# A four-layer graph attention kernel: counting and ranking of neighbour lists moved between engines

## The chip, the cores and the metric

The kernel runs on one core of a Trainium2 chip. A core has five engines that run side by side, each with its own in-order queue: TensorE (PE, matrix products into PSUM), VectorE (DVE), ScalarE (ACT), GpSimd (POOL) and SyncE (SP, which here only starts transfers). The metric is the device time of one execution in microseconds (us), as the median of several runs. A lower time is better.

## The reference

Four graph attention layers run one after the other on the same node features `x` (3327 nodes, 512 features) and the same graph `adj` (a 3327x3327 integer matrix, symmetric, with ones on the diagonal and about 0.5% of ones elsewhere). Every layer is preceded by a normalisation and a residual:

```python
h = jnp.maximum(_layernorm(x, axis=-1), 0.0)
x = x + _L0_gnn_ref(h, adj, L0_gnn_W, L0_gnn_a_src, L0_gnn_a_dst)
...
# inside a layer, for each head:
h = (x @ W.T).reshape(n, Hh, d)
e = leaky_relu(e_src[:, None, :] + e_dst[None, :, :], 0.2)
e = jnp.where(mask[:, :, None], e, -jnp.inf)
alpha = softmax(e, axis=1)
out = jnp.einsum('ijh,jhd->ihd', alpha, h)
```

The layers have 8, 4, 1 and 8 heads. A softmax row thus runs over the few neighbours of a node, and a kernel may gather those instead of multiplying with the whole matrix.

## The kernel before

The nodes are padded to 3328 and cut into 26 tiles of 128. A first stage, which fills about the first tenth of the time, builds for every node a list of up to 40 neighbours, sorts the nodes by the length of their lists, and makes the feature rows of layer 0. The four layers then work in the sorted order: tile t of the sorted nodes has a fixed number of list places (`CAPS[t]`), gathers that many rows with indirect transfers issued by GpSimd, weights them on VectorE and adds them up on TensorE. Only the first stage is touched by the change.

**The loop of the first stage** (`for t in range(NT)`, from L692) runs over the 26 tiles of `adj`. For tile t:

- SyncE loads the 128x3328 integers of `adj` into `a` (L697; three buffers). GpSimd multiplies them by descending column numbers into `key` (L698; three buffers), so that the largest keys are the first neighbours.
- VectorE raises the diagonal (L702) and takes the eight largest of each of 16 segments into `cand` (L707). ScalarE sums the row of `a` to the list length `total` (L704), writing the unneeded values into `waste`.
- Between VectorE's 16 segment operations the pieces of the tile before are run, one after each: five times "eight largest of the candidates" (`top`, L662) and four times their removal (L664); then `counted`, then `sorted_in`. After the ninth segment operation `placed` of the tile before that is run.
- `counted(t)`: ScalarE makes list entries from `top` (L632 `kept`, L633 `L`); VectorE counts the filled places into `held` (L635, an operation with an accumulator, which shows as two instructions).
- `sorted_in(t)`: VectorE compares the count with the 41 possible counts and gets a one-hot row `o` (L640); TensorE multiplies it by an upper triangle of ones and adds the counts so far, which gives the number of earlier nodes with the same count, `pn` (L642, L643), and updates the counts so far, `count` (L645, L646); ScalarE copies those to `sofar` (L649). `pn` and `count` have one PSUM buffer each.
- `placed(t)`: VectorE multiplies `pn` by `o` and sums, so that `part` holds the node's place within its count (L654).
- The feature rows: ScalarE's queue loads the tile of `x` into one of five row buffers `vx` (L726). ScalarE computes mean, centred features `xn`, sum of squares and `ve` (`centred_by_scalar`, L488 to L495; `xn` has two buffers). One tile later `features` makes the row: TensorE transposes `xn` (L454), ScalarE cuts at zero (`hT`, L461), TensorE multiplies by the weights (`pv`, L472, one buffer, eight products that the profile shows as sixteen), GpSimd takes the inverse square root of `ve` (`root`, L434), ScalarE scales `pv` into `vx` (L683, L685), and SyncE stores it into the table `tabx` (L687).

**The order.** On GpSimd and VectorE the order is that of the program text (a manual schedule). On ScalarE, TensorE and SyncE a scheduler orders the instructions before the run. On every engine the queue is then fixed, so an instruction that waits holds all behind it. On GpSimd the root of tile t-1 stands behind the key product of tile t. After the second tile VectorE folds the attention vectors into the weights (`W.fold`, L408, L410).

**The end of the stage**, after the last tile: VectorE forms from `count` the first place of every count (`base`, L738), multiplies all one-hot rows by it (L739, 128x1066), sums (L741), adds `part` (L742) and so has every node's rank. From the rank it makes selection matrices, with which TensorE sorts the lists (L789); the index lists (L790, L791) release the first gather of layer 0. `check` compares lengths and diagonals, for a dense path that these inputs never take.

## Time and profile before

| What | Value |
|---|---|
| median of 3 runs | 2420.67 us (2420.39 to 2422.86) |
| the profiled execution | 2419.54 us, span of its instructions 2417.8 us |
| mean granted clock of TensorE | 0.953 of full speed |
| busy: PE / DVE / ACT / POOL | 2068.3 / 1885.1 / 936.3 / 1739.5 us |
| first key product, last key product start | 5.2 us, 233.80 us |
| last `top` of the stage ends, ranks ready | 251.49 us, 256.7 us |
| first gather of layer 0 starts | 271.24 us |
| key product of GpSimd (L698), each | 7.26 us |
| row sum of `adj` on ScalarE (L704), each | 2.97 us |

The profile shows one execution. A line such as `L698 POOL ...` names a line of the kernel, the engine and the operation, and then the tile that it writes and those that it reads. A time in square brackets is the time that the engine was idle before the instruction, with the instruction or transfer that ended the wait. The waits view adds these up: which engine waited for which, the total in us, how many times, and the longest. The view by stretches gives the busy time of each engine in a piece of the execution, TensorE's granted clock, the busy share of the transfer engines and the rate. PEld is TensorE's loading of weights.

### The profile page before, as it was taken

To read this page: it belongs to the slowest core of one execution; us is meant where nothing else is said; L and a number is where in the kernel's file an instruction comes from. 1 tells how busy PE (TensorE), PEld (TensorE's weight loads), DVE (VectorE), ACT (ScalarE), POOL (GpSimd) and SP (SyncE) were. 2 spreads that over 40 slices of the span, in tenths; PEclk is the share of its full clock that TensorE was granted. 3 is DMA by queue.
4 is the path that set the end of the run, shared out by engine and by line. 5 is a ranking of instruction groups with operands and counts; after the bars stand their busy time and mean duration, and the time that the engine had idled before them with its cause. 6 is when DMAs were issued, how large, how long until landed. Compare 5 with 4: busy or idle time off the path is not lost.

```text
span 2417.8 us, 27489 instructions
## 1 busy us (share of the span) xinstructions
PE 2068.3 (86%) x7298; PEld 1197.0 (50%) x7298; DVE 1885.1 (78%) x4857; ACT 936.3 (39%) x2528; POOL 1739.5 (72%) x1717
## 2 busy tenths in 40 slices
PE   2778779888988885898999987899898699999997
PEld 1656334444444432454455544456565465556653
DVE  7988788877777763888888884888878578888886
ACT  5777113434331111433333332544443444344430
POOL 7899267777777776766677772778778467777775
PEclk9988899999999997999999998999999899999999
DMA  5887569999998788887888884889887578888885
GB/s 227 316 299 248 153 192 299 276 299 282 286 283 237 234 231 241 242 245 235 234 261 255 256 237 141 270 262 283 268 248 240 161 226 256 250 243 246 252 241 176
DMA packets 260732, 594.23 MB, mean 246 GB/s; under 512 B 103699, under 2 KB 121107, under 8 KB 256214
## 3 DMA queue, kind: packets, MB, share of 16 engines
q0 software_dynamic: 124368, 432.13, 59.5%
q1 hardware_dynamic: 132454, 153.45, 19.6%
q10 hardware_dynamic: 3744, 6.82, 0.8%
q8 instruction: 59, 0.97, 0.2%
q14 instruction: 107, 0.88, 0.1%
HBM read 542.60 MB, written 49.65 MB: 245 GB/s over the span
## 4 chain that ended last, share of the span: by engine, by line
DVE 31%; DMA 17%; PE 16%; issue 13%; POOL 12%; ACT 9%; DVEq 0%; SPq 0%; ACTq 0%; POOLq 0%
DVE m L931 13%; POOL g L838 8%; DMA g<-tab,idxb 6%; PE bank L936 5%; DMA g<-tabx,twiceb 4%; PE pv L472 4%; PE whole L1173 3%; POOL key L698 3%; DVE bank L924 3%; ACT r L1280 2%; DMA g<-tab,idxa 2%; DVE room L1296 2%; DVE z L902 2%; ACT pw L903 2%; DVE z L900 1%
## 5 line engine op out<-in xcount | busy, mean ns | idle before, releaser
L936 PE MATMUL bank<-m,ident 128*128 128x512 f32 x2414 | 1128.0, 613 | 144.8 <-DVE m L931 144.3
L838 POOL DMA_INDIRECT g<-tab,idxb x712 | 683.1, 959 | 236.0 <-issue 162.0
L931 DVE TENSOR_TENSOR m<-g,pw 128x512 f32<-128x512 f32 x1207 | 752.2, 682 | 100.2 <-ACT pw L903 99.6
L936 PEld LDWEIGHTS bank<-m,ident 128*128 128x128 f32 x2414 | 448.7, 194 | 689.2 <-issue 314.6
L472 PE MATMUL pv<-w,hT 128*128 128x264 f32 x1664 | 431.5, 413 | 67.8 <-ACT hT L461 44.5
L903 ACT ACTIVATE pw<-z 128x32 f32<-128x32 f32 (+4 forms) x356 | 68.2, 191 | 988.9 <-DVE z L902 988.9
L472 PEld LDWEIGHTS pv<-w,hT 128*128 128x128 f32 x1664 | 331.7, 203 | 166.8 <-ACT hT L461 50.8
L838 POOL DMA_INDIRECT g<-tab,idxa x297 | 286.3, 964 | 165.0 <-issue 110.6
L838 POOL DMA_INDIRECT g<-tabx,twiceb x342 | 324.0, 947 | 106.0 <-issue 79.5
L1173 PE MATMUL whole<-ve,em 128*128 128x512 f32 x468 | 217.8, 612 | 16.3 <-DVE em L1152 11.2
L698 POOL TENSOR_TENSOR key<-a,keys 128x3328 int32<-128x3328 int32 (+1 forms) x29 | 189.3, 6530 | 16.3 <-DVE cand L707 11.8
L924 DVE SCALAR_TENSOR_TENSOR bank<-g,L,bank 128x512 f32<-128x512 f32 x243 | 183.3, 754 | 6.8
L900 DVE TENSOR_TENSOR z<-g,pw 128x32 f32<-128x32 f32 (+4 forms) x356 | 62.6, 176 | 152.1 <-DMA g<-tabx,twiceb 64.7
L1314 PEld LDWEIGHTS whole<-L,room 128*128 128x128 f32 x1248 | 147.5, 190 | 24.9 <-issue 19.1
L838 POOL DMA_INDIRECT g<-tabx,twicea x99 | 94.9, 959 | 78.5 <-issue 38.1
L1314 PE MATMUL whole<-L,room 128*128 128x130 f32 x1248 | 147.8, 274 | 0.0
L707 DVE MAX8 cand<-key 128x8 f32<-128x208 int32 x416 | 144.0, 364 | 0.1
L1173 PEld LDWEIGHTS whole<-ve,em 128*128 128x128 f32 x468 | 88.1, 196 | 109.2 <-issue 87.2
L1280 ACT ACTIVATE r<-low,L 128x384 f32<-128x384 f32 x208 | 121.2, 583 | 5.1
L454 PE MATMUL pt<-ident,xn 128*128 128x128 f32 x416 | 65.4, 281 | 35.4 <-ACT hT L461 13.6
L454 PEld LDWEIGHTS pt<-ident,xn 128*128 128x128 f32 x416 | 52.5, 145 | 68.6 <-issue 28.3
L931 DVE TENSOR_TENSOR bank<-g,pw 128x512 f32<-128x512 f32 x74 | 51.5, 696 | 37.4 <-ACT pw L903 36.6
(180 smaller groups left out, 2192.6 us busy)
## 6 DMA issues: line engine op xcount, KB each, us to landing
a<-in_adj SPq DMA_DIRECT2D x25, 1664.0 KB
tab<-v SPq DMA_DIRECT2D x78, 264.0 KB
ve<-tab SPq DMA_DIRECT2D x78, 264.0 KB
g<-tab SPq DMA_DIRECT2D x65, 264.0 KB
tabx<-vx SPq DMA_DIRECT2D x26, 528.0 KB
g<-tab,idxb POOLq DMA_INDIRECT x712, 4.0
low<-tab SPq DMA_DIRECT2D x52, 132.0 KB
spare<-tab SPq DMA_DIRECT2D x52, 132.0 KB
```

Of the source, the lines that this page charges most:

```text
L454: nc.tensor.transpose(pt[:, k, :], xn[:, k * P:(k + 1) * P], ident)
L472: nc.tensor.matmul(pv[:, s, :HF + 8], hT[:, k, :], W.w[:, k, s, :], start=(k == 0), stop=(k == KC - 1))
L698: nc.gpsimd.tensor_tensor(key[:, c:c + quarter], a[:, c:c + quarter], keys[:, c:c + quarter], OP.mult)
L707: nc.vector.max(cand[:, g * 8:(g + 1) * 8], key[:, g * SEG:(g + 1) * SEG])
L838: nc.gpsimd.indirect_dma_start(out=out_, out_offset=None, in_=table, in_offset=bass.IndirectOffsetOnAxis(ap=which, axis=0))
L903: nc.scalar.activation(self.wt[:, k0:k0 + n, :H], z, AF.Exp)
L924: nc.vector.scalar_tensor_tensor(acc, v, w, acc, OP.mult, OP.add)
L931: nc.vector.tensor_tensor(out_.rearrange("p (s h d) -> p s h d", s=2, d=D), v.rearrange("p s (h d) -> p s h d", d=D), wt[:, k0 + q, :H].re ...
L936: nc.tensor.matmul(self.po, ident, m[:, q, :], start=False, stop=(k0 + q == K - 1), skip_group_check=True)
L1173: nc.tensor.matmul(tl.po.rearrange("p (s m) -> p s m", s=2), e[:, q * P:(q + 1) * P], v.rearrange("p (s m) -> p s m", s=2)[:, :, :F // 2], ...
L1280: nc.scalar.activation(self.r[:, h, :], self.a[:, g, :], AF.Relu, bias=-1.0, scale=self.b[:, j, g:g + 1])
L1314: nc.tensor.matmul(dst, e[:, h, q * P:(q + 1) * P], mov, start=False, stop=(j == NT - 1), skip_group_check=True)
```

## The change

ScalarE now counts the empty places instead of VectorE counting the filled ones: a second activation of `kept` with an accumulator, between `kept` and `L`. The possible counts `bins` run upwards, so that an empty count is compared with them. `sorted_in` comes two places later among VectorE's pieces. `placed` is now a copy by ScalarE of the whole `pn` into `before`, kept for all tiles, and at the end VectorE adds `base` to `before` for all tiles in one operation (128x1066), multiplies by `o` and sums. `features` of a tile runs two tiles later instead of one, for which `xn` has three buffers; the last two tiles' rows are made after the loop.

```diff
@@ centred_by_scalar
-    xn = work.tile([P, F], F32, name="xn")
+    xn = work.tile([P, F], F32, name="xn", bufs=3)
@@ tile_gat_stack
-        held = once.tile([P, NT], F32, name="held")
-        part = once.tile([P, NT], F32, name="part")
+        empty = once.tile([P, NT], F32, name="empty")
+        before = once.tile([P, NT, BINS], F32, name="before")
...
-            nc.scalar.activation(bins, counting(BINS, -1, KMAX, 0), AF.Copy)
+            nc.scalar.activation(bins, counting(BINS, 1, 0, 0), AF.Copy)
@@ counted
             nc.scalar.activation(kept, top, AF.Relu)
+            junk = small.tile([P, KMAX], F32, name="junk")
+            nc.scalar.activation(junk, kept, AF.Relu, scale=-1.0, bias=1.0, accum_out=empty[:, t:t + 1])
             nc.scalar.activation(L[:, t, :], kept, AF.Copy, scale=-1.0, bias=float(NP))
-            junk = small.tile([P, BINS], F32, name="junk")
-            nc.vector.scalar_tensor_tensor(junk[:, :KMAX], top, 0.0, one.to_broadcast([P, KMAX]), OP.is_gt,
-                                           OP.mult, accum_out=held[:, t:t + 1])
@@ sorted_in
-            nc.vector.tensor_scalar(o[:, t, :], bins, held[:, t:t + 1], None, OP.is_equal)
+            nc.vector.tensor_scalar(o[:, t, :], bins, empty[:, t:t + 1], None, OP.is_equal)
@@ placed
-            junk = small.tile([P, BINS], F32, name="junk")
-            nc.vector.scalar_tensor_tensor(junk, pn[:, :BINS], 1.0, o[:, t, :], OP.mult, OP.mult,
-                                           accum_out=part[:, t:t + 1])
+            nc.scalar.activation(before[:, t, :], pn[:, :BINS], AF.Copy)
@@ rest
             pieces.append(lambda: counted(t, top))
+            pieces += [lambda: None] * 2
             pieces.append(lambda: made.append(sorted_in(t)))
@@ check
-            nc.vector.tensor_tensor(m1, held, total, OP.not_equal)
+            nc.vector.tensor_tensor(m1, empty, total, OP.add)
+            nc.vector.tensor_scalar(m1, m1, float(KMAX), None, OP.not_equal)
@@ the loop over tiles
-        count, pieces, last, normed = None, [], None, None
+        count, pieces, last, normed = None, [], None, []
...
-                if normed is not None:
-                    features(*normed)
-                normed = (t, vx, *centred_by_scalar(nc, xt, small, work))
-            features(*normed)
+                if len(normed) == 2:
+                    features(*normed.pop(0))
+                normed.append((t, vx, *centred_by_scalar(nc, xt, small, work)))
+            for each in normed:
+                features(*each)
@@ the end
-            nc.vector.tensor_mul(o, o, base[:, :BINS].unsqueeze(1).to_broadcast([P, NT, BINS]))
+            nc.vector.tensor_tensor(before, before, base[:, :BINS].unsqueeze(1).to_broadcast([P, NT, BINS]), OP.add)
+            nc.vector.tensor_mul(o, o, before)
             rank = small.tile([P, NT], F32, name="rank", bufs=1)
             nc.vector.tensor_reduce(rank, o, AX.X, OP.add)
-            nc.vector.tensor_add(rank, rank, part)
```

## The prediction

> **What bounds the list building now.** The change touches only the first 260 us, so I left the page's totals and read that stretch: starts of the key products on GpSimd (L698), then the waits, then the timelines of ScalarE and TensorE. The page counts 26 products of about 7.26 us (the first cut in four); with the root (L434) a period of 7.73 us is the best GpSimd can do. Yet the one of tile 5 starts at 62.84 and that of tile 25 at 233.80: 8.55 us each. The waits from 60 to 245 us say why (engine line, awaited engine line: us, times, longest):
>
> ```profile
> ACT vx L683 <- PE pv L472: 15.8, 11, 5.3
> ...
> POOL key L698 <- DVE cand L707: 11.8, 1, 11.8
> ACT sofar L649 <- PE count L646: 11.6, 12, 2.3
> POOL root L434 <- ACT ve L495: 11.4, 6, 4.6
> ACT waste L488 <- DMA vx<-in_x: 10.9, 8, 2.3
> DVE junk L654 <- PE pn L643: 8.8, 7, 2.3
> ```
>
> The 11.8 is one wait at 62.8 us, for VectorE after it folded the weights; the change leaves it. What may go are 11.4 (GpSimd's in-order queue holds the next product behind a root that ScalarE feeds late) and 8.8 (VectorE held by the pick L654). I call "round t" VectorE's work between the diagonal additions (L702) of tiles t and t+1. Rounds 2 to 6 start at 55.64, 62.68, 69.71, 76.73 and 83.77, so an unheld round takes 7.03; rounds 23 and 25 start at 225.44 and 241.10.
>
> Two things in the trace decide what a new wait costs. VectorE's two counted operations are cheap in the stream:
>
> ```profile
> 61.29 0.18 DVE L635 SCALAR_TENSOR_TENSOR junk<-top,fixed 128x40 f32<-128x40 f32 x1
> 61.39 0.09 DVE L635 DVE_READ_ACCUMULATOR junk<-top,fixed 128x1 f32 x1
> 61.39 0.38 DVE L707 MAX8 cand<-key 128x8 f32<-128x208 int32 x1
> 61.68 0.24 DVE L640 TENSOR_SCALAR o<-fixed,held 128x41 f32<-128x41 f32 x1
> ```
>
> From start to start L635 delays what follows by 0.10 us, not by the 0.27 of its durations. And TensorE's clock halves when it resumes after a pause (columns: stretch, PE, PEld, DVE, ACT, POOL busy, clock, DMA share, GB/s):
>
> ```profile
> 82.11:85.53 3.42, 0.23 (x1) 0.23 (x2) 3.42 (x18) 3.42 (x7) 3.42 (x1) 1.00 0.95 395
> 85.53:88.94 3.41, 3.41 (x12) 2.77 (x11) 2.62 (x14) 2.66 (x9) 3.13 (x3) 0.50 1.06 332
> 109.42:112.83 3.41, 3.07 (x18) 2.75 (x18) 3.41 (x18) 3.41 (x6) 3.29 (x3) 1.00 0.94 386
> ```
>
> [...] the weight products (L408) on VectorE last 6.88 and 7.36 us beside a key product, and 0.70 without.
>
> **The change, part by part.** VectorE loses L635 and L654: 0.10 us each by start-to-start, so a round takes 6.83. ScalarE gains the empty count (taken as L632's 0.23 us, plus a 0.19 accumulator read) and the copy of the prefix counts (as L649, 0.20). In the stream, where starts follow at about 0.13, 0.09 and 0.11, that is 0.33 us a tile; neither form is in the trace, so at worst it is their whole 0.62, and it can't be a gain, being added work. I take 0.33. The end work gains an addition of 128x1066.
>
> The root a tile later takes GpSimd's wait for ve away. But VectorE's one-hot (o) now waits for ScalarE's count, and what stands ahead of that count decides. The scheduler's order of the changed ScalarE queue, once steady, is:
>
> ```
> sofar, before, xn, hT, squares, waste(a), kept, vx (528), empty, L, vx (16), ve, mean of x, load x
> ```
>
> TensorE's order is: one product of pv, then pn and count, seven of pv, four transposes. Thus a ring: o -> pn, count -> sofar -> before -> xn -> hT -> squares -> waste(a) -> kept -> vx -> empty -> o. Its length, start to start, from this ScalarE row and others like it:
>
> ```profile
> 94.59 0.61 ACT L488 ACTIVATE waste<-vx 128x512 f32<-128x512 f32 x1
> 95.11 0.19 ACT L488 ACTIVATION_READ_ACCUMULATOR waste<-vx 128x1 f32 x1
> ...
> 96.79 0.21 ACT L649 ACTIVATE sofar<-count 128x41 f32<-128x41 f32 x1 [1.37 <-PE count L646]
> 96.90 0.71 ACT L490 ACTIVATE xn<-vx,nm 128x512 f32<-128x512 f32 x1
> 97.51 2.97 ACT L704 ACTIVATE waste<-a 128x3328 bf16<-128x3328 int32 x1
> 100.38 0.19 ACT L704 ACTIVATION_READ_ACCUMULATOR waste<-a 128x1 f32 x1
> 100.47 0.69 ACT L683 ACTIVATE vx<-pv,root 128x528 f32<-128x528 f32 x1
> ```
>
> ScalarE: sofar 0.10, before 0.12, xn 0.61, hT 0.48, squares 0.61, waste(a) 2.96, kept 0.13, vx 0.58: 5.59. From the empty count back to sofar there are two branches. By VectorE: 0.37 to o, 0.3 to pn, about 1.0 through count: 1.7. By TensorE: pv has one buffer, so its first product waits for vx (16), which starts 0.36 after the count; 0.32 on it begins, and pn stands behind it:
>
> ```profile
> 64.74 0.71 PE L472 MATMUL pv<-w,hT 128*128 128x264 f32 x2 [0.70 <-ACT vx L685]
> 65.29 0.31 PE L642 MATMUL pn<-o,upper 128*128 128x41 f32 x2
> ```
>
> so 0.36 + 0.32 + 0.55 + 1.03 = 2.26. The longer branch gives 5.59 + 2.26 = 7.85 us a tile at full clock, already over GpSimd's 7.73. TensorE works 5.3 of it and pauses 2.5 just before pv and pn, where half clock strikes. In the kernel before, TensorE's bursts after 64 us last 5.15 warm; of nine that follow a pause over 2.2 us seven ran at half clock (6.7 to 9.3 us), and of those after 1.76 or less none as a whole. A cold burst is 1.7 longer, so its next pause is short and the clock stays up: about every second tile is cold. Then pn to count takes 1.77 instead of 1.0 (from 191.5 us), and pv's first product up to 0.5 more. Half the tiles with 0.9 more: 0.45. Ring: 8.3. (No cold tile: 7.85; all cold: 8.75.) The mean of x sits in a 1 us hole of the ring, so a load of x of up to 8.8 us is hidden; landings here take 2.5 to 8.6.
>
> First rounds. In round 1 the count stands behind waste(a) and xn, and VectorE reaches the folding about 0.9 late; [...]: nothing [...]. In round 2 the count stands behind vx of tile 1, which waits for pv until 63.70:
>
> ```profile
> 63.70 0.70 ACT L683 ACTIVATE vx<-pv,root 128x528 f32<-128x528 f32 x1 [5.28 <-PE pv L472]
> ```
>
> o can start at 63.70 + 0.6 + 0.37 = 64.7; unheld it would at 62.15. Round 3 starts at 65.2, +2.5. Round 3 is not held: 72.0, +2.3. In round 4 the count stands behind waste(a), which waits for xn of tile 5; its load is issued at about 69, not at 66.3, and I take 5 us: x at 74, count at 80.4, round 5 at 81.2, +4.5. Round 5 is held 0.9: round 6 at 89.0, **+5.2**. (A load of 3 us: +3.5; cold TensorE: +6.5.) While VectorE is late GpSimd waits for its key buffers (three), as at 62.84: no reserve catches this.
>
> Then 17 rounds on the ring, 17 x 8.3 = 141.1, against 225.44 - 83.77 = 141.7: **-0.6**. Rounds 23 and 24 have no waste(a) left: 2 x 6.83 against 15.66: **-2.0**.
>
> The end. The last count goes by ScalarE: the last top is done at 251.49, o follows at 251.77; now 0.04 + 0.27 + 0.33 + 0.04 = 0.68 instead of 0.28: +0.4. The 1066-wide addition costs what L739 does, 1.27, with its gap 1.30; L654 and the addition of ranks go, 0.23 and 0.22 from start to start; round 25 saves 0.2: +0.65. Together **+1.05**. One more small operation of the check fits into the 0.77 that the scan waits for count. Loads, stores and GpSimd's issues are as many as before; stores of rows go a tile later, and in SP's queue a load of adj then stands behind an older store, so it's hidden by the three buffers. Moves of SBUF addresses I cost at nothing.
>
> Sum: 5.2 - 0.6 - 2.0 + 1.05 = +3.7. The profiled execution took 2419.54 (span 2417.8), so 2423.2 for it; the median of the runs, 2420.67, is 1.1 higher: **2424.4 us**. 0.2% is 4.8 us, and that bounds the three chances.
>
> **Rivals.** *GpSimd is freed (faster).* For it: 11.4 + 8.8 of waits are named to it and to VectorE, and both lose their cause. If half clock misses the ring (7.85 a tile), the 17 rounds take 133.5, -8.2, and the sum is -3.9: 2416.8; if the ring hides behind GpSimd's 7.73 and the early load lands soon, -8: 2412.7. Against: the pause falls ahead of pn. It decides below 8.05 a tile. *TensorE cold everywhere (slower).* The pause of every ring triggers half clock, which at 174 to 181 us lasted two windows: 8.75 a tile, +7.1 instead of -0.6: sum +11.4, 2432. For it: 2.5 us of pause each time; against: a cold burst runs longer and leaves a shorter pause, so warm and cold alternate. *The wait is only exchanged (no change).* Ring 8.1, sum about 0: 2420.9.
>
> **Chances.** Ring at 8.2 to 8.5: 0.45, less than half of it beyond +4.8. Exchanged, 8.0 to 8.2: 0.17. Freed: 0.18. Cold everywhere: 0.20. So slower 0.43, same 0.38, faster 0.19. The range takes in freed and most of cold: 2414 to 2432; of the likeliest alone, 2420 to 2428.
>
> **What would show it.** VectorE's L639 should wait for ScalarE by 0.5 to 1.5 us in most rounds; GpSimd's root should wait for nothing, and its key for VectorE's cand; sofar should wait for count in every tile; round 3 should start near 65.2, round 6 near 89, and rounds then come every 8.3; the end from last top to rank should be 1.1 longer. Wrong if L639 doesn't wait (the order leaves more slack than I think), if rounds come at 7.8 (clock), or if the mean of x waits for its load again.

## The result, and the profile after

The changed kernel is slower, by more than the prediction's range allowed.

| What | Before | After |
|---|---|---|
| median | 2420.53 us (2418.01 to 2422.86, 6 runs) | 2434.97 us (2431.39 to 2437.87, 6 runs) |
| ratio after / before | | 1.0057, 95% interval 1.0046 to 1.0067 |
| the profiled execution, its span | 2419.54, 2417.8 us | 2433.78, 2432.1 us |
| round 6 starts | 83.77 us | 90.59 us |
| rounds 6 to 22, each | 8.33 us | 8.52 us |
| rounds 23 and 24 together | 15.66 us | 17.74 us |
| start of round 25 to ranks ready | 15.63 us | 18.22 us |
| ranks ready, first gather | 256.73, 271.24 us | 271.47, 287.10 us |

The ranks come 14.74 us later and the profiled execution ends 14.24 us later: all of the loss arises in the list building. Its parts, each a difference of two entries above, are 6.82 us up to round 6, 3.25 in the next 17 rounds together, 2.08 in rounds 23 and 24, and 2.59 at the end.

The waits of the kernel after, from 60 to 245 us (engine line, awaited engine line: us, times, longest):

```profile
DVE o L639 <- ACT junk L634: 35.4, 20, 3.1
ACT waste L488 <- DMA vx<-in_x: 18.2, 14, 2.5
POOL key L697 <- DVE cand L706: 14.3, 1, 14.3
ACT sofar L648 <- PE count L645: 13.1, 11, 2.7
...
ACT vx L682 <- PE pv L472: 7.1, 6, 2.7
```

The first line is the new wait: VectorE waits for ScalarE's count in 20 rounds, 1.8 us each time. (The expectations below speak of 39.5 us; that is the same wait counted up to 255 us.) GpSimd's 11.4 us for ve and VectorE's 8.8 us for pn, which stood in this view before, are gone, as the change meant. But ScalarE's waits for loads of x, 10.9 us before, are now 18.2.

The ring of one tile, in ScalarE's timeline after (start, duration, engine line operation, and in brackets the idle time before it):

```profile
83.78 0.21 ACT L648 ACTIVATE sofar<-count 128x41 f32<-128x41 f32 x1 [2.73 <-PE count L645]
...
83.97 0.72 ACT L490 ACTIVATE xn<-vx,nm 128x512 f32<-128x512 f32 x1
...
85.67 2.98 ACT L703 ACTIVATE waste<-a 128x3328 bf16<-128x3328 int32 x1
...
89.18 0.70 ACT L682 ACTIVATE vx<-pv,root 128x528 f32<-128x528 f32 x1 [0.31 <-PE pv L472]
...
89.78 0.23 ACT L634 ACTIVATE junk<-kept 128x40 f32<-128x40 f32 x1
89.91 0.19 ACT L634 ACTIVATION_READ_ACCUMULATOR junk<-kept 128x1 f32 x1
90.00 0.22 ACT L635 ACTIVATE L<-kept 128x40 f32<-128x40 f32 x1
```

The count (L634) costs ScalarE 0.22 us from start to start, and stands at the end of the chain that the prediction described: 6.00 us after sofar, of which 0.31 is a wait for products; the prediction had 5.59. The 2.73 us before sofar are more than foretold. Most of it comes from TensorE's clock: from pn to the end of count takes 1.77 us in this tile instead of 1.0. Besides, two products of pv stand ahead of pn in this early tile instead of one, 1.92 us. The clock, in the view by stretches (stretch, then PE, PEld, DVE, ACT and POOL busy, clock, DMA share, GB/s):

```profile
75.14:78.55 3.41, 0.79 (x5) 0.42 (x4) 3.05 (x13) 3.38 (x4) 3.41 (x1) 1.00 0.98 390
78.55:81.96 3.41, 1.90 (x4) 1.50 (x5) 1.70 (x8) 2.51 (x11) 3.32 (x3) 0.51 0.42 107
81.96:85.38 3.42, 3.42 (x13) 3.05 (x12) 3.42 (x19) 1.60 (x5) 3.42 (x1) 0.50 1.04 416
85.38:88.79 3.41, 3.41 (x9) 2.59 (x8) 1.77 (x7) 3.41 (x5) 3.41 (x2) 0.50 0.66 276
88.79:92.20 3.41, 2.49 (x17) 2.02 (x16) 2.07 (x10) 2.18 (x12) 1.40 (x2) 0.99 0.90 277
```

After a stretch with 0.79 us of products the clock is at half for three stretches.

Where the rounds ended, round 23, the count was late in another way. ScalarE's and VectorE's timelines:

```profile
243.52 0.70 ACT L682 ACTIVATE vx<-pv,root 128x528 f32<-128x528 f32 x1 [2.70 <-PE pv L472]
244.12 0.27 ACT L684 ACTIVATE vx<-pv,root 128x16 f32<-128x16 f32 x1
244.28 0.72 ACT L490 ACTIVATE xn<-vx,nm 128x512 f32<-128x512 f32 x1
...
245.66 0.22 ACT L634 ACTIVATE junk<-kept 128x40 f32<-128x40 f32 x1
...
246.00 0.26 DVE L639 TENSOR_SCALAR o<-fixed,empty 128x41 f32<-128x41 f32 x1 [4.06 <-ACT junk L634]
```

There is no row sum of `adj` left here, and still VectorE waits 4.06 us: the count stands behind the feature row of an older tile, and that row waits for its products. TensorE's clock was at half from 235.6 to 242.5 us.

### The profile page after: what moved, and what is told of

It reads as the page before. It is cut to its first block, busy times and chain, and to the rows that moved or that the text cites. A ratio compares the mean times of both kernels' runs of the same rounds, so it can differ in the third digit from the quotient of the medians.

```text
span 2432.1 us, 27476 instructions
## 1 busy us (share of the span) xinstructions
PE 2080.9 (86%) x7298; PEld 1207.0 (50%) x7298; DVE 1879.4 (77%) x4754; ACT 943.5 (39%) x2606; POOL 1743.2 (72%) x1717
## 3 DMA queue, kind: packets, MB, share of 16 engines
q10 hardware_dynamic: 3744, 6.82, 0.8%
## 4 chain that ended last, share of the span: by engine, by line
DVE 25%; DMA 14%; issue 11%; PE 10%; ACT 9%; POOL 8%; DVEq 0%; SPq 0%; ACTq 0%; POOLq 0%
DVE m L931 11%; POOL g L838 7%; DMA g<-tab,idxb 6%; DMA g<-tabx,twiceb 4%; PE bank L936 4%; ACT r L1280 3%; PE pv L472 3%; PE whole L1173 2%; DVE bank L924 2%; DMA g<-tab,idxa 2%; DVE room L1296 2%; ACT pw L903 1%; DVE z L902 1%; DVE z L900 1%; DVE x L974 1%
## 5 line engine op out<-in xcount | busy, mean ns | idle before, releaser
L706 DVE MAX8 cand<-key 128x8 f32<-128x208 int32 x416 | 139.0, 362 | 0.1
```

The source lines that it names most:

```text
L706: nc.vector.max(cand[:, g * 8:(g + 1) * 8], key[:, g * SEG:(g + 1) * SEG])
```

## The experiments

Eighteen kernels ran. Every ratio is to the kernel before, on the same chip. None of them leaves out work; two add useless products.

### Which part of the change costs the time

**Rows alone.** The kernel before, with features two tiles later and three buffers of `xn`:

```diff
-                if normed is not None:
-                    features(*normed)
-                normed = (t, vx, *centred_by_scalar(nc, xt, small, work))
-            features(*normed)
+                if len(normed) == 2:
+                    features(*normed.pop(0))
+                normed.append((t, vx, *centred_by_scalar(nc, xt, small, work)))
+            for each in normed:
+                features(*each)
```

> The kernel before with one part of the change alone: a tile's feature row is made two tiles later, with three buffers of xn. Ring theory (the 14 us were lost because VectorE's one-hot waits for ScalarE's count, in a ring that also holds late loads of x and slow products): no ring here, the one-hot waits for nothing but VectorE itself; GpSimd's root has ve early, so part of its 11.4 us goes: 2412 to 2421 us. Rival (the later rows cost the time: a row buffer is held a tile longer, so its next load of x starts late): 2428 us or more, with ScalarE's mean of x waiting for its load as often as in the changed kernel (18 us).

Measured: 0.9994 (0.9981 to 1.0007), no difference that can be told. The rival is out as a cost: the wait that it named is there (23.2 us of ScalarE for loads of x), the time isn't. Nor is the gain that the theory allowed: GpSimd still waits 17.2 us for ve, more than the 11.4 of the kernel before.

**The count given back to VectorE.** The changed kernel, with this undone (`bins` and `check` follow):

```diff
-            junk = small.tile([P, KMAX], F32, name="junk")
-            nc.scalar.activation(junk, kept, AF.Relu, scale=-1.0, bias=1.0, accum_out=empty[:, t:t + 1])
+            junk = small.tile([P, BINS], F32, name="junk")
+            nc.vector.scalar_tensor_tensor(junk[:, :KMAX], top, 0.0, one.to_broadcast([P, KMAX]), OP.is_gt,
+                                           OP.mult, accum_out=held[:, t:t + 1])
-            pieces += [lambda: None] * 2
```

> The changed kernel with its count given back to VectorE: later rows and the copied prefix counts stay, the one-hot follows its count on VectorE at once. Ring theory: VectorE's waits for ScalarE's count (39.5 us in the changed kernel) are gone and nothing takes their place in full, 2413 to 2421 us; the end costs about 1 us of it. Rival (later rows): still 2430 us or more. Rival (the copies of prefix counts and the wide addition at the end): as the end is priced at 1.3 us and the copies at 0.12 us a tile, at most 2425 us.

Measured: 0.9989 (0.9982 to 0.9997), median 2418.61 us, in the ring theory's range. Against the changed kernel's 1.0057 this is some 16 us less, from the count (with its two empty places) alone. Its waits from 60 to 245 us:

```profile
ACT waste L488 <- DMA vx<-in_x: 20.8, 11, 4.3
DVE key L700 <- POOL key L696: 13.8, 14, 2.6
POOL root L434 <- ACT ve L495: 13.0, 4, 6.3
...
ACT sofar L649 <- PE count L646: 11.2, 8, 4.1
```

ScalarE waits for loads of x as much as in the changed kernel, and it does little harm: of what hangs on ScalarE only GpSimd's root still shows, with 13.0 us in four waits. VectorE waits for GpSimd only, whose product and root are the bound once its lead is used up; rounds 6 to 22 take 7.70 us each. Round 25 starts at 230.09 us, 11 earlier than before, but the ranks come only 1.5 us earlier (255.22), of which more below.

**The later rows taken away.** The changed kernel with `features` one tile later, as before (the core of the edit; `xn` has two buffers again):

```diff
-                if len(normed) == 2:
-                    features(*normed.pop(0))
+                if normed is not None:
+                    features(*normed)
```

> The changed kernel with the rows made one tile later again as before: count on ScalarE and copied prefix counts stay. Ring theory: VectorE still waits for ScalarE's count by 30 us or more, and GpSimd waits for ve besides: 2430 to 2445 us. Rival (later rows cost the time): back to 2419 to 2424 us.

Measured: 1.0063 (1.0048 to 1.0078); from 60 to 245 us VectorE waits 36.0 us for the count (35.4 in the changed kernel), GpSimd 13.6 for ve. So no cost or gain of the later rows can be told beside the count.

**More slack for the count.** The changed kernel, with the one-hot of a tile among the next tile's pieces (the core of the edit):

```diff
-            pieces += [lambda: None] * 2
-            pieces.append(lambda: made.append(sorted_in(t)))
-            return pieces, lambda: placed(t, made[0])
+            return pieces, lambda: made.append(sorted_in(t)), lambda: placed(t, made[0])
...
+                if older is not None:
+                    pieces.insert(3, older[0])
```

> The changed kernel with the one-hot of a tile taken one round later, so that ScalarE's count has some 5 us more; all of the changed kernel's operations stay, in number and size. Ring theory: the wait of the one-hot for ScalarE shrinks from 39.5 to under 8 us, the rounds come every 7.8 to 8.1 us instead of 8.5, 2414 to 2424 us. Rival (ScalarE simply has more work than a round holds): the waits move to ScalarE's other customers and the rounds stay at 8.4 us or more, 2430 us or more. Rival (later rows): likewise 2430 or more.

Measured: 1.0073 (1.0050 to 1.0097). The expectation of the time fell. The slack did shorten the middle: rounds 6 to 22 take 8.22 us each instead of 8.52, though VectorE still waits 31.8 us for the count. But from the start of round 25 to the ranks it takes 26.4 us instead of 18.2 (VectorE's wide addition waits 5.46 us for the last copy of prefix counts), and round 6 starts 1.8 us later. ScalarE's order is the scheduler's, and in the early rounds it moved the count back. ScalarE's and VectorE's timelines:

```profile
75.72 0.63 ACT L488 ACTIVATE waste<-vx 128x512 f32<-128x512 f32 x1 [7.10 <-DMA vx<-in_x]
...
77.10 0.22 ACT L634 ACTIVATE junk<-kept 128x40 f32<-128x40 f32 x1
...
77.44 0.26 DVE L639 TENSOR_SCALAR o<-fixed,empty 128x41 f32<-128x41 f32 x1 [4.36 <-ACT junk L634]
```

Here the count stands behind a mean of x that waits 7.10 us for its load. An edit in the program text does not fix what stands ahead of an instruction here; so the next kernels write the orders out.

### What stands in the ring

**Orders written out.** ScalarE and TensorE join the manual schedule; all operations are the changed kernel's. In the round of tile t, ScalarE does the mean, xn, squares and ve of tile t-1, hT of tile t-2, the row sum of tile t, kept, empty count and list of tile t-1, the row of tile t-2, the load of x of tile t+2, and sofar and before of tile t-1. TensorE does the eight products of tile t-2, then pn and count of tile t-1, then the next four transposes.

```diff
-        with tc.manual_schedule(engines={mybir.EngineType.Pool, mybir.EngineType.DVE}):
+        with tc.manual_schedule(engines={mybir.EngineType.Pool, mybir.EngineType.DVE, mybir.EngineType.PE,
+                                         mybir.EngineType.Activation}):
...
+                hT = turn(due[0], due[2]) if due else None
...
                         nc.scalar.activation(waste, a, AF.Relu, accum_out=total[:, t:t + 1])
+                        if due:
+                            pv = project(hT)
...
+                    if g == 11 and due:
+                        row(due[0], due[1], pv, rstd)
+                        load(t + 2)
```

> All operations of the changed kernel, but ScalarE's and TensorE's orders are written out: in ScalarE's queue the count of empty places follows right on the kept list and stands ahead of the feature row, x is loaded two tiles ahead, the products of a row stand together on TensorE, and only the last row is left for the end. Ring theory (what costs is what stands in the ring through ScalarE's count: the row and its slow products, late loads): the ring shrinks to sofar, before, mean, xn, squares, ve, hT, row sum, kept, count, o, pn, count = about 7.8 us, rounds of 7.8 to 8.1, 2413 to 2422 us. Rival (counting on ScalarE costs the time wherever it stands, by its own work or its semaphores): rounds of 8.4 or more, 2430 us or more.

Measured: 1.0113 (1.0097 to 1.0128). The rounds come in a pattern of 8.05, 9.55 and 9.55 us, 9.03 in the mean. TensorE's timeline, and then ScalarE's, of the same two tiles:

```profile
157.16 5.51 PE L472 MATMUL pv<-w,hT 128*128 128x264 f32 x16 [2.76 <-ACT hT L461]
...
166.72 3.83 PE L472 MATMUL pv<-w,hT 128*128 128x264 f32 x16 [2.76 <-ACT hT L461]
```

```profile
162.77 0.70 ACT L686 ACTIVATE vx<-pv,root 128x528 f32<-128x528 f32 x1 [2.10 <-PE pv L472]
...
170.64 0.70 ACT L686 ACTIVATE vx<-pv,root 128x528 f32<-128x528 f32 x1 [0.41 <-PE pv L472]
```

The same sixteen products take 5.51 or 3.83 us, and as sofar stands behind the row on ScalarE, the difference of 1.7 is most of what tells a long round from a short one (1.5). I had left this second loop (hT, products, row, sofar) out of the expectation. The numbers are those of the rival, but neither of the two theories describes what bounds this kernel.

**The row ahead of the count.** The same, with the row between `kept` and the count:

```diff
             nc.scalar.activation(kept, top, AF.Relu)
+            if between:
+                between.pop()()
```

> The kernel with the written-out orders, with one thing put back: ScalarE makes the older tile's feature row between the kept list and the count of empty places, as in the changed kernel. Ring theory: the count now waits for the row (0.7 us) and for its eight products when these run at half clock (up to 1.7 us more); 0.7 to 1.5 us a tile over the kernel with the written-out orders, 14 to 30 us more in all, and VectorE waits for ScalarE's count by 20 us or more. Rival (the place of the row doesn't matter, only loads do): within 4 us of it.

Measured: 1.0377 (1.0363 to 1.0391), 64 us more than without. The direction is as expected and the size twice the largest guess: from 60 to 245 us VectorE waits 77.2 us for the count and ScalarE 48.0 for the products (43.8 and 30.2 without), since now the products, the count, the one-hot and pn all follow one another.

**A load of x one tile ahead.**

```diff
-                        load(t + 2)
...
+                load(t + 1)
                 vx = rows[t % 5]
```

> The kernel with the written-out orders, with one thing put back: x is loaded one tile ahead of its use instead of two. Late-load theory: a landing takes 2.5 to 8.8 us and a round 7.8, so the mean of x waits in several tiles and its wait is in the ring: 3 to 9 us more than with two tiles. Rival (loads land behind other work, as the prediction had it): within 2 us.

Measured: 1.0163 (1.0147 to 1.0179), 12 us more than with two tiles. The size was a little above the theory's, the cause another: no mean of x waits for a load in this trace. The rounds are 8.26 and 9.80 instead of 8.05 and 9.55: 0.2 more in each, and more of the long ones. The load's issue, 0.33 us in ScalarE's queue, has moved from the wait for the products to a place where nothing hides it; that this is the 0.2 us is a reading of the two traces.

**The same orders with the count on VectorE.** The edit is that of the second experiment, on the written-out orders.

> The same written-out orders with the count on VectorE as before, and the later rows and copied prefix counts of the change kept. Theory: no ring through ScalarE; rounds of 6.9 us as long as GpSimd's lead of three buffers lasts and GpSimd's 7.8 after it; ranks at about 247 us against 256.7 before, of which the transfers of the first gathers may give some back: 2408 to 2415 us. Rival (the list stage's end doesn't reach the end of the kernel): 2417 us or more.

Measured: 1.0081 (1.0067 to 1.0095). The expectation fell: rounds 6 to 22 take 8.98 us each. From 60 to 245 us ScalarE waits 33.8 us for products and VectorE 34.9 for GpSimd's keys. GpSimd's waits for ve come to 19.0 us, but 16.3 of them are a single wait at 65 us; what held its later products the trace doesn't settle.

**More work between products and row.** hT goes behind the mean of x (`then` below), and the row sum is taken a tile ahead:

```diff
     nc.scalar.activation(waste, xt, AF.Copy, scale=-1.0 / F, accum_out=nm)
+    if then is not None:
+        then()
...
-                        nc.scalar.activation(waste, a, AF.Relu, accum_out=total[:, t:t + 1])
+                        for n, each in [(0, a), (1, ahead_of[0])] if t == 0 else [(t + 1, ahead_of[0])] if t + 1 < NT else []:
...
+                            nc.scalar.activation(waste, each, AF.Relu, accum_out=total[:, n:n + 1])
```

> All operations of the changed kernel, in orders written out anew. In the earlier written-out orders ScalarE waited for a row's eight products in every tile (32 us, 8.05 us a tile with full clock, 9.55 with half clock), because only the row sum of adj stood between their start and their use. Now the activation that feeds the products stands right behind the mean of x, five us of other work ahead of the row, and the row sum is taken a tile early. Ring theory: the ring through the count, without rows, late loads and products, is about 8.0 us whatever TensorE's clock, 0.5 us a tile less than in the changed kernel, and GpSimd's 7.8 is just below it: 2416 to 2426 us, ScalarE waits for the products by under 5 us, VectorE for the count in most tiles. Rival (the count on ScalarE costs by itself): 2430 or more.

Measured: 1.0051 (1.0037 to 1.0065). ScalarE's wait for the products has fallen from 30.2 to 15.5 us, not to 5. Rounds alternate between 7.91 and 9.1 us, 8.45 in the mean, and VectorE still waits 33.4 us for the count.

> The same orders, later rows and copied prefix counts, with the count on VectorE as before the change. Theory: no ring through ScalarE at all; rounds of 6.9 us while GpSimd's lead of three key buffers lasts, then GpSimd's 7.8; the ranks come 5 to 10 us earlier than before: 2409 to 2417 us. Rival (the list stage is bound by another loop that both orders share, through the buffers of adj or ScalarE's own work): as slow as its sister with the count on ScalarE.

The same orders with the count on VectorE: 1.0007 (0.9998 to 1.0016), some 10 us faster than its sister. VectorE waits for no count of ScalarE, as the theory said; the time it promised does not come. The rounds take 8.32 us each, in which the issue of a load of x stands in ScalarE's queue until the row's store has freed its buffer (16.9 us in all, in 10 waits; that this is what lengthens the rounds is not shown). And the end is longer.

That holds for all six kernels with written-out orders so far: from the start of round 25 to the ranks they take 24.1 to 26.9 us, against 18.2 in the changed kernel and 15.6 in the kernel before. In the first of them the last one-hot waits 6.98 us for its count. So compared with the changed kernel their times hold 6 to 9 us that arise behind the rounds, and of the ring only their rounds tell.

### The changed kernel's own order, and its two suspects

These four write out the steady order that the scheduler had made for the changed kernel. The base first. Of its diff the emission of a tile is the core (`wide` and `narrow` are the two parts of a row; `between` runs behind `kept` and behind the list; the last row is made behind the last count):

```diff
+                centre(t)
+                cutting(t - 1)
+                turn(t)
+                squares = square(t)
...
+                    between.append(lambda t=t: wide(t - 2))
...
+                        narrow(t - 2)
+                    variance(t, squares)
+                    mean(t + 1)
+                    load(t + 1 + 1)
...
+                            project(t - 1, products[:1])
...
+                    project(t - 1, products[1:])
```

> The changed kernel's steady order of ScalarE and TensorE, written out by hand for every tile, as the base for the next two: sofar, before, xn, hT, squares, row sum, kept, row, count of empty places, list, small row part, ve, mean of x, load of x one tile ahead; one product, pn and count, seven products, four transposes. Only the last rows differ (the last one is made behind the last count). Ring theory: rounds of 8.3 to 8.7 us as in the changed kernel, VectorE waits for the count by 30 us or more, 2428 to 2438 us.

> The same with six row buffers instead of five and x loaded two tiles ahead. Late-load theory: ScalarE's mean of x no longer waits for its load (under 3 us in all), and what it pushed the counts by goes: 4 to 10 us less than the run with one tile ahead. Rival (half clock is what lengthens the ring, loads wait in a hole): within 2 us of it.

```diff
-        rows = [once.tile([P, 2 * ROW], F32, name=f"vx{i}") for i in range(5)]
+        rows = [once.tile([P, 2 * ROW], F32, name=f"vx{i}") for i in range(6)]
...
-                    load(t + 1 + 1)
+                    load(t + 1 + 2)
```

> The same order with one tile ahead and five buffers, and eight useless products of 128x128 on TensorE between a tile's transposes and the next row's first product, where TensorE otherwise pauses; they write a bank that is not in use then. Half-clock theory: the clock of the stage stays near full, the alternation of short and long rounds goes, 5 to 12 us less than without the filling, though TensorE does more. Rival (late loads): within 2 us, or more time, as the filling delays the count.

```diff
                 turn(t)
+                if t > 3:
+                    fill = ps_i.tile([P, BANK], F32, name="pi")
+                    for i in range(8):
+                        nc.tensor.matmul(fill[:, :P], ident, ident, start=True, stop=True)
```

> The hand-written copy of the changed kernel's steady order with both: six row buffers and x loaded two tiles ahead, and eight useless products in TensorE's pause. Theory (late loads and half clock lie in the same hole of the ring, and each hides the other): rounds of 7.8 to 7.9 us nearly everywhere, VectorE's wait for the count under 20 us, 2418 to 2424 us, 8 to 12 us less than with one of them. Rival (the ring is held by something else): 2428 us or more, rounds of 8.3 or more.

| Kernel | ratio (95%) | median us | rounds 6 to 22, each | clock, 100 to 200 us | ranks ready |
|---|---|---|---|---|---|
| base | 1.0046 (1.0034 to 1.0058) | 2432.00 | 8.52 | 0.81 | 269.23 us |
| x two tiles ahead | 1.0048 (1.0036 to 1.0060) | 2432.31 | 8.50 | 0.81 | 268.86 us |
| pause filled | 1.0040 (1.0028 to 1.0052) | 2430.58 | 8.49 | 0.94 to 0.97 | 265.89 us |
| both | 1.0025 (1.0017 to 1.0034) | 2426.09 | 8.50 | 0.93 to 0.95 | 266.41 us |

The base reproduces the changed kernel: rounds of 8.52 us, VectorE's wait 36.0 against 35.4. Its rounds alternate between 7.8 and 9.27 us, with a mean clock of about 0.95 in the short and 0.67 in the long. The waits of the four, in the order of the table, from 60 to 245 us:

```profile
DVE o L643 <- ACT junk L636: 36.0, 21, 2.7
...
ACT sofar L652 <- PE count L649: 18.0, 18, 2.2
ACT waste L700 <- DMA vx<-in_x: 13.7, 15, 1.8
```

```profile
DVE o L643 <- ACT junk L636: 35.5, 21, 2.7
ACT sofar L652 <- PE count L649: 32.7, 20, 2.2
...
ACT sofar L652 <- DMA tabx<-vx: 1.3, 1, 1.3
```

```profile
DVE o L643 <- ACT junk L636: 33.1, 21, 3.2
...
ACT waste L700 <- DMA vx<-in_x: 22.1, 17, 2.3
ACT sofar L652 <- PE count L649: 8.4, 8, 2.2
```

```profile
DVE o L643 <- ACT junk L636: 33.3, 21, 3.2
...
ACT sofar L652 <- PE count L649: 20.1, 16, 2.2
ACT sofar L652 <- DMA tabx<-vx: 12.9, 6, 3.1
```

Read the second and third waits of each block together: 31.7, 34.0, 30.5 and 33.0 us. ScalarE has one hole in the ring, around the mean of x and ahead of sofar, and something always fills it. Some of it belongs to the ring: with x two tiles ahead, sofar waits 0.92 us for count in nearly every short round, and 2.20 in nearly every long one. Loads taken away, the count of half-clocked products fills it. The clock kept up, loads fill it, though they take no longer (7.8 us in the median from issue to landing, 8.2 in the base; the profile holds the landing of five and six of them). Both taken away, the issue of a load, which waits for a row's store, takes a good part. So taking the late loads away alone gave nothing (the rival's number), and keeping the clock up alone gave little. The useless products have a price too: in round 8 of the last kernel they still run when the row is ready, and hold the next first product by some 0.3 us. With both, the theory's time came only in part (4 to 6 us less than with one of them, not 8 to 12) and its rounds not at all: 8.50 instead of 7.8 to 7.9. Of the 6 us to the base, the ranks explain 2.8: up to round 6 (1.3) and in rounds 23 and 24 (1.3), nearly nothing between. The rest arises behind the list building and is not explained; the two kernels ran on different chips. That the waits replace each other in one hole is shown. That the whole ring would come at 7.8 with all of them gone wasn't tried; single rounds do (7.80 in rounds 22 and 23 of the last kernel, at full clock and with no wait for a load or a store).

### The last rows

**Rows behind the last count.** The changed kernel, and then the version with VectorE's count:

```diff
-            for each in normed:
-                features(*each)
             pieces[4:4] = [last]
             for piece in [*pieces, check, then]:
                 piece()
+            for each in normed:
+                features(*each)
```

> The changed kernel with one thing moved: the feature rows of the last two tiles are written in the program behind the last tile's count and prefix counts instead of ahead of them. Tail theory: in the changed kernel the last counts stand behind rows that wait for half-clocked products (waits of 4.06 and 0.85 us in the last rounds, 1.3 at the scan), so the ranks come about 3 to 6 us earlier: 2429 to 2432 us. Rival (the first gather needs those rows, so they only move to where it waits for them): 2434 us or more.

Measured: 1.0059 (1.0045 to 1.0073), the changed kernel's own ratio. The last one-hots wait for the count by 0.86 and 0.66 us as before, and the scan 1.30. The traces show why: the move in the program text left the order of work on every engine as it was, so neither the tail theory nor the rival was tested. What the run does give is a profile of a second execution of the changed kernel's orders. In it round 6 starts at 92.85 us (90.59 in the first), rounds 6 to 22 take 8.47 (8.52), rounds 23 and 24 16.08 (17.74), and the ranks come at 271.2 (271.5). The single parts of the loss thus differ by about 2 us between executions, while their sum hardly does.

> The kernel with the count on VectorE, later rows and copied prefix counts, and the last two tiles' rows behind the last prefix counts. With those rows ahead of them its rounds ended 11 us before those of the kernel before (230.1 against 241.1 at tile 25), but its ranks only 1.3 us, because the last list and counts stood behind three rows. Tail theory: most of these 8 us come back, ranks at 246 to 250 us, 2409 to 2414 us. Rival (the rows are what the first gathers wait for): 2417 to 2420 us as with the rows ahead.

Measured: 0.9990 (0.9980 to 0.9999), as without the edit, which is the rival's time. The ranks did come 2.9 us earlier (252.31), but VectorE then waited 4.1 us for the small product of `check`, which stood behind the last row's products on TensorE.

**The last row behind that product.**

```diff
+            features(*normed.pop(0))
...
             nc.vector.tensor_copy(bad, worst)
+            features(*normed.pop(0))
+            nc.sync.dma_start(tabx[:NP, :].rearrange("(t p) c -> p t c", p=P)[:, :, F // 2:F // 2 + 1],
+                              rank.unsqueeze(2))
```

> The count on VectorE, later rows and copied prefix counts, with the last row's products behind the product of the check at the end, and the ranks stored behind that row. In the version with both last rows ahead of it that product stood behind the last row's products and held VectorE 4.1 us. Tail theory: VectorE goes on at once, the first gather comes some 4 us earlier than at 271.0, 2412 to 2417 us, faster than both kernels. Rival (the last row's products now hold the selection's products instead): 2418 us or more.

Measured: 0.9968 (0.9958 to 0.9978), median 2415.32 us, faster than both kernels. Yet the profile does not show what was expected. The end of its list building, on several engines (SPq is SyncE's queue):

```profile
261.02 0.32 SPq L685 DMA_DIRECT2D tabx<-vx  x1
264.13 0.37 SPq L759 DMA_DIRECT2D tabx<-rank  x1
266.31 0.27 ACT L789 ACTIVATE idxa<-pi 128x120 int32<-128x120 f32 x1 [5.32 <-PE pi L788]
...
270.91 1.19 POOL L837 DMA_INDIRECT g<-tabx,twicea  x1 [26.42 <-PE pi L788]
```

VectorE and TensorE are 4 us earlier (the index list is written at 266.31, in the kernel before at 270.38), but the ranks are stored behind the last row, at 264.13, and the gather starts at 270.91 against 271.24. That the gather waits for this store, and not for the index list that the view names, is my reading. The profiled execution is the longest of this kernel's fourteen (2423.11, the others 2410 to 2420), so where the faster ones win is open, and the tail theory has its time but not its cause.

**One row fewer at the end.** VectorE's count, the rows one tile later from tile 20 on:

```diff
-                if len(normed) == 2:
+                while len(normed) >= (2 if t < 20 else 1):
                     features(*normed.pop(0))
```

> The count on VectorE, copied prefix counts, rows two tiles later up to tile 19 and one tile later from tile 20 on, so that a single row is left for the end, behind the last prefix counts and ahead of the check's product. Tail theory (the last rows hold the ranks, or the ranks' store holds the gather): ranks at 246 to 252 us and the first gather 3 to 6 us earlier than at 271, 2411 to 2416 us. Rival (the extra row at tile 20 throws ScalarE back by as much): 2417 us or more and the first gather at 270 us or later.

Measured: 1.0001 (0.9990 to 1.0012). The rival held: from the extra row on, one round takes 16.01 us and a later one 11.59, in which VectorE waits for GpSimd's keys and GpSimd's root for ScalarE, and the first gather starts at 272.76.

## Why the prediction was wrong

**The mechanism was right in the main.** The one-hot waits for ScalarE's count, through the ring that was described, and from 60 to 245 us GpSimd's root waits for nothing. The experiments bear it out: without the count on ScalarE the loss is gone, without the later rows it stays. ScalarE waits for count in 11 tiles, not in every tile as foretold, because waits for x fill the same hole in others. What failed are terms that lengthen the ring.

**First rounds: right, on the dearer branch.** In round 1 VectorE started its first weight product (L408) 0.65 us later than before (30.06 against 29.41; 0.9 foretold), yet that product ended at 31.59 instead of 32.03, and round 2 started at 55.45 instead of 55.64: the price of nothing, an estimate of mine, held. Round 3 started at 64.97 (65.2 foretold), round 4 at 71.76 (72.0), round 5 at 80.72 (81.2). Round 6 came at 90.59, where 89.0 was the forecast and +6.5 the price "if TensorE cold": it was cold, with sofar waiting 2.73 us.

**"A load of x of up to 8.8 us is hidden": the step that failed in the middle.** The 17 rounds took 8.52 us each, 3.25 more in all where 0.6 less was forecast. The shortest of them, such as rounds 6, 20 and 22, took 7.80, near the 7.85 of the ring at full clock. What exceeds 7.80 comes to 12.3 us, and the rounds divide in two. Four ran largely at half clock (13, 15, 19 and 21, mean clock 0.61 to 0.70) and took 9.08 to 9.97: 6.4 us of it. The price for half clock had been 0.45 a round, 7.7 in all, so it was about right in sum, though by luck: fewer rounds than "every second tile", at 1.6 us each instead of 0.9. The other 5.9 us arise at a mean clock of 0.79 and more, where the mean of x waits for its load. Round 8, on TensorE and ScalarE:

```profile
107.34 0.39 PE L645 MATMUL count<-sofar,ident 128*128 128x41 f32 x2
108.11 0.63 ACT L488 ACTIVATE waste<-vx 128x512 f32<-128x512 f32 x1 [1.87 <-DMA vx<-in_x]
...
108.82 0.21 ACT L648 ACTIVATE sofar<-count 128x41 f32<-128x41 f32 x1
```

The count was ready at 107.73, and sofar starts 1.09 us later, behind the mean of x. The load had been issued at 100.32, so 7.8 us were not hidden. In the rounds that it lengthened, the load came 7.8 to 9.4 us after its issue. The prediction had put this term at nothing, as 1 us of hole on a ring of 7.85; but the load is issued behind the mean of the tile before, so it has less. The reading that landings take at most 8.6 us was wrong too. In the kernel before, a mean that waited for its load started 9.2 us after the issue:

```profile
122.44 0.34 ACTq L726 DMA_DIRECT2D vx<-in_x  x1
...
131.61 0.63 ACT L488 ACTIVATE waste<-vx 128x512 f32<-128x512 f32 x1 [0.81 <-DMA vx<-in_x]
```

The prediction had named a mean of x that waits again as a sign of being wrong, and that sign came, in 14 tiles. It doesn't follow that earlier loads would have saved the 5.9 us. In the hand-written base nearly every second round is a long one, at half clock, and most waits for x lie inside those; there the loads could be taken away without any gain.

**"Rounds 23 and 24: no waste(a) left, -2.0": wrong, +2.1.** This and the 17 rounds are the largest misses, 4.1 and 3.9 us. I had taken the row sum for what delays the count there. The trace shows a row of an older tile ahead of it, waiting 2.70 us for half-clocked products. The clock is 0.76 from 200 to 240 us, against 0.88 and 0.84 in the two stretches of 50 us before. In the second execution of the same orders the two rounds took 16.08 us, and in the hand-written base 16.03, instead of 17.74. So some 1.7 us of this miss can differ from one execution to the next, and the rest, +0.4 instead of -2.0, is the wrong step.

**"The end: +1.05": +2.59.** The addition itself was priced rightly (1.30 from start to start). Missing were the waits of the last one-hots for the count (0.85 and 0.66) and of the scan for count, 1.29 against 0.77 before.

**The rivals.** "TensorE cold everywhere" came nearest, with 2432, but not for its cause: the clock was at 0.84 to 0.88 in the middle rounds, and four of the 17 ran largely at half. "GpSimd is freed" is what the kernel with VectorE's count does, at 7.70 us a round.

## What to carry to other kernels

When a counter moves from the engine that uses it to another in-order engine, price everything that stands ahead of it in that queue, with the waits of those instructions, not the counter itself: here the count costs ScalarE 0.22 us and the kernel some 16. Where two or three late things meet in one hole of a ring, removing one only uncovers the next, so a wait's total isn't its price. And a stage whose rounds get faster may win little: here the rounds ended 11 us earlier and the kernel won 2.7, with the last rows, counts and stores still to come. Last, look whether an edit of the program text has changed an engine's order at all before its time is read.

## What the runs showed of the hardware

- **Half clock can outlast a busy stretch.** In the changed kernel's trace from 55 to 300 us the clock changes on steps 3.41 us apart. Of the stretches between them 15 are busy for 98% or more at half clock (0.50 or 0.51); full clock (0.99) follows on 11 of them, and another stretch at half on four. One of the four is that from 81.96 to 85.38 us, busy throughout at 0.50; the next, busy too, is at 0.50 still. What tells them apart is open.
- **A pause can be filled.** Eight useless 128x128 products per tile raised the mean clock from 100 to 200 us from 0.81 to 0.96 (0.94 with six row buffers), and that of the whole execution from 0.943 to 0.956 in both.
- **A small transfer can take almost as long as a large one.** From 100 to 240 us the changed kernel's loads of x (256 KB) took 7.7 us in the median from issue to landing, those of `adj` (1664 KB) 8.7; in the kernel with VectorE's count, 4.8 and 9.2. (The profile holds the landing of five to seven of each.) A load of x is issued on ScalarE's queue and one of `adj` on SyncE's; what makes the difference between 7.7 and 4.8 us no run here shows.
- **An issue waits like any instruction.** Loads of x whose buffer was still being stored held ScalarE's queue for 12.9 us in all in one kernel (six waits) and 16.9 in another (ten).
